# Four chained image layers on one core: channel squares added on GpSimd, row lengths sent through DRAM, first tokens moved among the first row's units

## The chip, the core and the metric

One core of one Trainium2 chip runs the whole program. The metric is device microseconds (us) for one execution, the median of several; lower is better. The engines are TensorE (PE, with its weight loads as PEld), VectorE (DVE), ScalarE (ACT), GpSimd (POOL) and SyncE (SP), which issues almost all DMAs of this kernel.

## The reference, cut to what matters

Four images of 56 x 56 tokens with 256 channels pass through four layers, each `x = x + layer(groupnorm(x))`. Layers 0, 2 and 3 are windowed attentions. The change lies in layer 1, a graph step in which every token of an image looks at every other one:

```python
x  = groupnorm(x)                                  # per image, n = 3136 tokens, c = 256
xn = x / maximum(norm(x, axis=-1), EPS)            # each token to unit length
A  = einsum('bnc,cc,bmc->bnm', xn, W_adj, xn)      # n x n per image
A  = exp(5 * (A - max(A)));  A = A * (1 - eye(n))
A  = A / maximum(sum(abs(A)), EPS)
xW = einsum('bnc,dc->bnd', x, W_aff)
diff = rowsum * (xW + b_aff) - A @ x @ W_aff.T
y  = leaky(layernorm(diff) * ln_gamma + ln_beta)   # then x = x + y
```

## The kernel before: tiles, queues and hand-written order

Data is float32 and lies with channels on partitions, as two halves of 128 channels (`CC = 2`). Layer 1 cuts an image into 24 tiles of 128 tokens and a rest of 64. Token preparation works on chunks of four tiles (512 tokens): chunks 0 to 5, and chunk 6, which holds the rest of this image (128 columns). The product A is symmetric, so only its upper triangle is made: a row `j` of tiles is a sequence of units `(b, j, first, last)` of up to four tiles. One unit is: logits (`logits`, L1409, 128x512), exponential (L1412, ACT), transposes (L1500, copied at L1503), and for each tile one product by row (L1514, summed in PSUM over the row) and one by column (L1519), which DVE adds to `acc` (L1441). Units of the rest have no `j` (L1451, L1470, L1480, L1484).

Preparing one chunk is the function `tokens(b, c)`, which returns steps:

- `load` (L1347): DMA of the chunk from DRAM to `x0`.
- `normal(h)` for both channel halves: group normalisation on DVE (L939), and after the second half the square of both halves on ACT (L1356, 128x1024), which overwrites `x0`.
- `values(i0)`: tokens times `W_aff` on PE (L1377), two tiles at a time, copied to `xw` by ACT (L954) and DVE (L952) in turn.
- `lengths`: the sum of squares of each token, by 1-column matmuls of the squares with ones, one for each tile and each channel half (L1364); then a floor on DVE (L1366), the power -1/2 on POOL (L1367) and a diagonal matrix `dg` on POOL (L1368).
- `unit_length`: one 128x512 matmul of ones with `dg` (L1385), which leaves each token's reciprocal length on all partitions, and the multiplication into `xnT` on DVE (L1387). `scaled(j)` (L1402, POOL) then makes the weighted tile `xd` for row j.

Where these steps stand is written by hand. Layer 1 runs under a manual schedule for PE and DVE: both execute in exactly the order in which the Python code issues the work[...]. ACT, POOL and SP are put in order by a scheduler. Three lists drive it:

- `small`: entries (when, step, chunk). `small_step` is called twice in each unit and runs the first entry whose `when` is not above `done`, the count of tiles processed.
- `ticks`: steps run one at a time after a product by column, behind the `due` steps of finished rows (L1573, L1578).
- `ready(chunk)`: called before a step of a chunk is taken from `small`; it issues at once whatever of the chunk's two `normal` steps still waits in `ticks`.

For images 1 to 3, `replace(b + 1, c)` is called at the start of rows 3, 6, 10, 14, 16, 19 and 23 of the image before (for chunks 6, 0, 1, 2, 3, 4, 5). It issues the load, appends four empty ticks and the two `normal` steps to `ticks`, and puts the other steps at the front of `small`:

```python
ticks.extend([no_step] * 4 + normals[b, c])
small[:0] = [(done + 12, step, (b, c)) for step in steps]
# steps: values(0), lengths, values(2), unit_length
```

For image 0 all seven chunks are prepared ahead of the first unit, in a loop, with PSUM tiles borrowed from tags v, o, t and s. Two rest units come first, then row 0. At the end of layer 0 the SP queue also fetches tables for layer 2: `w_wqkv` (L881, 768 KB) and two halves of `bias` (L1726, 3024 KB each).

Of the kernel before, what the change touches and what calls it, by code (L numbers as in the profile page):

```python
# [24 lines left out]
FP = mybir.dt.float32  # L25
I32 = mybir.dt.int32
AF = mybir.ActivationFunctionType
ALU = mybir.AluOpType
# [3 lines left out]
NIMG = 4  # L32
# [3 lines left out]
P = 128  # L36
CC = C // P
# [14 lines left out]
TINY = 1e-12  # L52
# [778 lines left out]
def direct_blocks(ctx: ExitStack, tc: tile.TileContext, d: dict, watch):  # L831
# [3 lines left out]
    nc = tc.nc  # L835
    const = ctx.enter_context(tc.tile_pool(name="dconst", bufs=1))
    dram = ctx.enter_context(tc.tile_pool(name="ddram", bufs=1, space=bass.MemoryType.DRAM))
    ps = None
    no_step = lambda: None
# [16 lines left out]
    ident = const.tile([P, P], FP, name="ident")  # L856
    make_identity(nc, ident)
    ones = const.tile([P, P], FP, name="ones")
    nc.vector.memset(ones, 1.0)
    mhalf = const.tile([P, CC], FP, name="mhalf")  # L860
# [9 lines left out]
    def psum_tile(tag, bufs, banks=1):  # L870
        shape = [P, 512] if banks == 1 else [P, banks, 512]
        return ps.tile(shape, FP, tag=tag, name="ps_" + tag, bufs=bufs)
# [447 lines left out]
    def layer1(early, big, pool, late, next_layer):  # L1320


        NB, REST = divmod(T, P)
        NC4 = NB // 4
# [5 lines left out]
        xnT = big.tile([P, CC, (NB + 1) * P], FP, name="xnT")  # L1330
        xw = big.tile([P, NB + 1, C + 1], FP, name="xw")
        xdr = big.tile([P, CC, P], FP, name="xdr")
        offd = big.tile([P, P], FP, name="offd")
        nc.vector.tensor_scalar(offd, ident, -1.0, 1.0, ALU.mult, ALU.add)
        nc.vector.memset(xw[:, :, C:], -1.0)

        def tokens(b, c, ps_a=ps_m):

            tiles = range(4 * c, min(4 * c + 4, NB + 1))
            k, m = P, len(tiles)  # L1340
            n = m * P
            box = {}

            def load():
                x = box["x0"] = early.tile([P, CC, 512], FP, tag="x", name="x1")
                if c < NC4:
                    nc.sync.dma_start(out=x[:, :, :n], in_=tokens_of(1, b, 4 * c * P, n))  # L1347
                else:
                    for i in range(2):
                        nc.sync.dma_start(out=x[:, :, i * REST:(i + 1) * REST], in_=tokens_of(1, b, NB * P, REST))  # L1350
                box["x"] = early.tile([P, CC, 512], FP, tag="xn", name="xn1")

            def normal(h):
                normalise(box["x"][:, h, :n], box["x0"][:, h, :n], known(1, b), h)
                if h:
                    nc.scalar.activation(box["x0"][:, :, :n], box["x"][:, :, :n], AF.Square)  # L1356

            def lengths():
                pm, sq = ps_a(), box["x0"]
                rn = early.tile([P, 4, 1], FP, tag="rn", name="rn")  # L1360
                dg = box["dg"] = early.tile([P, 4, P], FP, tag="dg", name="dg", bufs=1)
                for i, t in enumerate(tiles):
                    for h in range(CC):
                        nc.tensor.matmul(pm[:k, i:i + 1], lhsT=sq[:, h, i * P:i * P + k], rhs=ones[:, 0:1],  # L1364
                                         start=(h == 0), stop=(h == CC - 1))
                nc.vector.tensor_scalar_max(rn[:k, :m, 0], pm[:k, :m], TINY * TINY)  # L1366
                nc.gpsimd.tensor_tensor(rn[:k, :m, 0], rn[:k, :m, 0], mhalf[:k, 0:1].to_broadcast([k, m]), ALU.pow)  # L1367
                nc.gpsimd.tensor_tensor(  # L1368
                    dg[:k, :m, :k], ident[:k, :k].rearrange("p (o q) -> p o q", o=1).to_broadcast([k, m, k]),
                    rn[:k, :m, :].to_broadcast([k, m, k]), ALU.mult)  # L1370

            def values(i0):
                pm = ps_a()
                mm = min(2, m - i0)
                for i in range(i0, i0 + mm):
                    for h in range(CC):
                        nc.tensor.matmul(pm[:k, (i - i0) * C:(i - i0 + 1) * C], lhsT=box["x"][:, h, i * P:i * P + k],  # L1377
                                         rhs=w_aff[:, h, :], start=(h == 0), stop=(h == CC - 1))
                evac(i0 // 2, xw[:k, 4 * c + i0:4 * c + i0 + mm, :C],
                     pm[:k, :mm * C].rearrange("p (a b) -> p a b", b=C))  # L1380

            def unit_length():

                pm = ps_a()
                nc.tensor.matmul(pm[:, :n].rearrange("p (m k) -> p m k", k=k), lhsT=ones[:k, :], rhs=box["dg"][:k, :m, :k],  # L1385
                                 start=True, stop=True)
                nc.vector.tensor_tensor(xnT[:, :, 4 * c * P:4 * c * P + n], box["x"][:, :, :n],  # L1387
                                        pm[:, :n].rearrange("p (o k) -> p o k", o=1).to_broadcast([P, CC, n]), ALU.mult)
                if c == NC4:
                    for h in range(CC):  # L1390
                        nc.gpsimd.tensor_scalar_mul(xdr[:, h, :], xnT[:, h, NB * P:], adj[:, h:h + 1])

            return [load], [lambda h=h: normal(h) for h in range(CC)], [lambda: values(0), lengths] + [lambda i=i: values(i) for i in range(2, m, 2)] + [unit_length]

        xd, out, xr = {}, {}, {}
        y_rest = late.tile([REST, C + 1], FP, name="yr", bufs=1)

        def scaled(j):

            xd[j] = pool.tile([P, CC, P], FP, tag="xd", name="xd", bufs=3)  # L1400
            for h in range(CC):
                nc.gpsimd.tensor_scalar_mul(xd[j][:, h, :], xnT[:, h, j * P:(j + 1) * P], adj[:, h:h + 1])  # L1402
# [206 lines left out]

        units = []  # L1610
        for b in range(NIMG):
            if b == 0:
                units += [(b, None, q) for q in range(2)]
            for j in range(NB):
                units += [(b, j, i, min(i + 4, NB)) for i in range(j, NB, 4)]
                if j == 0:
                    units.append((b, None, 2))
                if b + 1 < NIMG and 0 <= j - 20 < 2:
                    units.append((b + 1, None, j - 20))
        turn = iter(range(6 * (NC4 + 1)))  # L1620
        fresh = [tokens(0, c, lambda: psum_tile(*(("v", 2), ("o", 2), ("t", 1), ("s", 2))[next(turn) % 4])) for c in range(NC4 + 1)]
        for c in range(2):
            fresh[c][0].pop()()
        for step in fresh[0][1]:
            step()
        for c in range(NC4 + 1):
            for step in (fresh[c + 1][1] if c < NC4 else []) + fresh[c][2]:
                step()
            if c + 2 <= NC4:
                fresh[c + 2][0].pop()()  # L1630
        small, done = [], 0

        normals = {}

# [6 lines left out]
        def small_step():  # L1641
            for i, (when, step, chunk) in enumerate(small):
                if when <= done:
                    small.pop(i)
                    if chunk and chunk != -1:
                        ready(chunk)
                    return step()
            step_stats()
# [8 lines left out]
        def replace(b, c):  # L1657
            if b < NIMG:
                for item in [a[2] for a in small if a[2] not in (None, -1)]:
                    now(item)  # L1660
                (load,), normals[b, c], steps = tokens(b, c)
                load()
                ticks.extend([no_step] * 4 + normals[b, c])
                small[:0] = [(done + 12, step, (b, c)) for step in steps]

        def begin(w):
            if w[1] is None:
# [7 lines left out]
        e = begin(units[0])  # L1675
        for k, w in enumerate(units):
            b, j, first = w[:3]
            if first == j:
                residual(b, j * P // CH)
                residual(b, j * P // CH + 1)  # L1680
                if j in begin_at:
                    replace(b + 1, begin_at[j])
                if (b, j) == (NIMG - 2, 8):
                    small += [(done + 20, step, None) for step in next_layer()]
            small_step()
            at = transposed(*w, e) if j is not None else rest_transposed(e[0])
            if k + 2 < len(units) and units[k + 2][1] == units[k + 2][2]:
                scaled(units[k + 2][1])
            ahead = begin(units[k + 1]) if k + 1 < len(units) else None
            small_step()  # L1690
            if j is None:
                rest_products(b, first, *e, at)
                done += 4
                if first == NC4 // 2 - 1:
                    last_add = finish(b, NB)
            else:
                products(*w, e, at)
                done += w[3] - first
                if w[3] == NB:
                    finish(b, j)  # L1700
            e = ahead
# [555 lines left out]
```

## Time and profile before

| | |
|---|---|
| median of 3 runs | 3989.01 us |
| lowest and highest run | 3976.07 and 3992.41 us |
| profiled execution: span, first to last instruction | 3977.8 us |
| mean granted TensorE clock in the span | 0.983 |
| PE busy in the span | 3814.5 us (96%) |
| DVE, POOL, ACT busy in the span | 2372.2, 1745.8, 1381.2 us |
| layer 1: first to last matmul, about | 803 to 2754 us |
| 880 to 2700 us: PE busy | 1809.5 of 1820 us |

No separate total is given for the profiled execution; its span is 1.7 us above the lowest timed run and 11.2 us below the median. In rows of the profile, a time such as `1.00` under PEclk is the granted clock as a share of full speed, `xN` is the number of instructions, and `[a <-E tile Lnnn]` is idle time of that engine before the instruction and what ended it. A float32 matmul is recorded as two instructions[...], so eight 1-column matmuls show as x16.

### The profile page before, as it was taken

To read this page: it belongs to the slowest core of one execution; us is meant where nothing else is said; L and a number is where in the kernel's file an instruction comes from. 1 tells how busy PE (TensorE), PEld (TensorE's weight loads), DVE (VectorE), ACT (ScalarE), POOL (GpSimd) and SP (SyncE) were. 2 spreads that over 40 slices of the span, in tenths; PEclk is the share of its full clock that TensorE was granted. 3 is DMA by queue.
4 is the path that set the end of the run, shared out by engine and by line. 5 is a ranking of instruction groups with operands and counts; after the bars stand their busy time and mean duration, and the time that the engine had idled before them with its cause. 6 is when DMAs were issued, how large, how long until landed. Compare 5 with 4: busy or idle time off the path is not lost. (4 is left out here: it accounts for less than half of the span.)

```text
span 3977.8 us, 92350 instructions
## 1 busy us (share of the span) xinstructions
PE 3814.5 (96%) x38871; PEld 2707.4 (68%) x38871; DVE 2372.2 (60%) x4431; ACT 1381.2 (35%) x2927; POOL 1745.8 (44%) x1883
## 2 busy tenths in 40 slices
PE   7999999889999999999999999999999999899998
PEld 4566666557777677776777767776676666566765
DVE  6777777734345544445444553446788887666665
ACT  3455545422222222222222222222555555344443
POOL 3566767721123312233112331123677777555554
PEclk9899999989999999999999999999999999999999
DMA  8343333320000100001000000001344443434442
GB/s 270 104 134 119 113 120 104 99 104 1 24 19 24 40 6 15 20 25 35 6 24 15 25 24 10 10 10 56 111 125 126 125 121 111 157 120 135 127 128 93
DMA packets 268659, 301.84 MB, mean 76 GB/s; under 512 B 25926, under 2 KB 260584, under 8 KB 267752
## 3 DMA queue, kind: packets, MB, share of 16 engines
q1 hardware_dynamic: 267946, 295.76, 23.9%
q8 instruction: 308, 5.05, 0.5%
q14 instruction: 117, 0.96, 0.1%
q10 hardware_dynamic: 288, 0.08, 0.0%
HBM read 203.39 MB, written 92.37 MB: 74 GB/s over the span
## 5 line engine op out<-in xcount | busy, mean ns | idle before, releaser
L1441 DVE TENSOR_TENSOR acc<-acc,ps_v 128x257 f32<-128x257 f32 x1104 | 463.4, 423 | 718.7 <-PE ps_v L1519 690.7
L1519 PE MATMUL ps_v<-xw,e 128*128 128x257 f32 x2208 | 612.6, 382 | 1.2 <-DVE acc L1441 1.2
L1514 PE MATMUL ps_o<-xw,at 128*128 128x257 f32 x2208 | 609.0, 379 | 0.0
L1409 PE MATMUL ps_s<-xnT,xd 128*128 128x512 f32 (+3 forms) x1344 | 572.7, 549 | 3.9 <-DVE xnT L1387 3.9
L1519 PEld LDWEIGHTS ps_v<-xw,e 128*128 128x128 f32 x2208 | 413.5, 189 | 142.7 <-issue 82.4
L1503 ACT COPY at<-ps_t 128x512 f32<-128x512 f32 (+3 forms) x332 | 170.6, 514 | 970.0 <-PE ps_t L1500 969.7
L1078 POOL TENSOR_TENSOR b<-e 126x336 f32<-126x336 f32 (+5 forms) x512 | 500.0, 997 | 9.6 <-ACT e L1066 1.5
L1514 PEld LDWEIGHTS ps_o<-xw,at 128*128 128x128 f32 x2208 | 419.1, 190 | 60.1
L945 PE MATMUL ps_m<-xn,w_wqkv 128*128 128x392 f32 x1024 | 379.1, 504 | 12.3 <-DVE dv L922 3.9
L1402 POOL TENSOR_SCALAR xd<-xnT,vec 128x128 f32<-128x128 f32 x192 | 116.8, 619 | 569.3 <-PE ps_s L1409 565.7
L1069 POOL TENSOR_TENSOR e<-e,m0t 126x672 f32<-126x672 f32 (+3 forms) x128 | 238.6, 1864 | 265.8 <-ACT e L1068 245.4
L1069 POOL TENSOR_TENSOR e<-e,bias 119x784 f32<-119x784 f32 (+5 forms) x128 | 244.0, 1906 | 179.9 <-ACT e L1068 178.6
L1409 PEld LDWEIGHTS ps_s<-xnT,xd 128*128 128x128 f32 x1344 | 225.8, 191 | 141.8 <-issue 126.5
L1412 ACT ACTIVATE e<-ps_s 128x512 f32<-128x512 f32 x336 | 185.4, 552 | 347.8 <-PE ps_s L1409 340.8
L990 ACT ACTIVATE no<-rs 128x168 f32<-128x168 f32 (+2 forms) x256 | 93.8, 367 | 583.8 <-DVE rs L1841 268.3
L945 PEld LDWEIGHTS ps_m<-xn,w_wqkv 128*128 128x128 f32 x1024 | 187.8, 191 | 137.3 <-ACT pr L2097 17.5
L1087 PEld LDWEIGHTS ps_o<-e,vp 124*32 124x32 f32 (+3 forms) x8192 | 177.8, 111 | 147.4 <-issue 97.7
L1087 PE MATMUL ps_o<-e,vp 124*32 124x112 f32 (+3 forms) x8192 | 242.0, 254 | 6.2 <-POOL e L1069 4.4
L1841 DVE RECIPROCAL rs<-ps_o 128x196 f32<-128x196 f32 (+2 forms) x128 | 176.0, 1375 | 87.1 <-PE ps_o L1087 86.6
L939 DVE TENSOR_SCALAR xn<-x,gst 128x28 f32<-128x28 f32 (+4 forms) x368 | 207.5, 616 | 32.3 <-PE ps_m L945 22.9
L1066 ACT ACTIVATE e<-e 126x672 f32<-126x672 f32 (+5 forms) x256 | 219.5, 857 | 20.7 <-DVE e L1065 8.0
L1019 POOL TENSOR_TENSOR e<-e,m3l 98x784 f32<-98x784 f32 x64 | 118.3, 1848 | 217.9 <-ACT e L1016 217.9
(196 smaller groups left out, 6293.8 us busy)
## 6 DMA issues: line engine op xcount, KB each, us to landing
x<-xr SPq DMA_DIRECT2D x64, 392.0 KB
x<-in_x SPq DMA_DIRECT2D x53, 448.0 KB
x<-x SPq DMA_DIRECT2D x60, 392.0 KB
xr<-x SPq DMA_DIRECT2D x60, 392.0 KB
vd<-v SPq DMA_DIRECT2D x72, 256.0 KB
xr<-in_x SPq DMA_DIRECT2D x32, 392.0 KB
xr<-x SPq DMA_DIRECT2D x28, 448.0 KB
x<-xr SPq DMA_DIRECT2D x28, 448.0 KB
```

Of the source, the lines that this page charges most:

```text
L939: nc.vector.tensor_scalar(dst, src, gst[:, h, 0:1], gst[:, h, 1:2], ALU.subtract, ALU.mult)
L945: nc.tensor.matmul(pm[:, :n], lhsT=w[:, h, col:col + P], rhs=rhs(h), start=(h == 0), stop=(h == CC - 1))
L1066: nc.scalar.activation(ev, ev, AF.Exp)
L1069: nc.gpsimd.tensor_tensor(parts(ev), parts(ev), w["emask"], ALU.mult)
L1078: nc.gpsimd.tensor_tensor(w["b"][a][:nk, :, :2 * nq].rearrange("p h (i c) -> p h i c", i=2), ev[:, :, :, 0, :], ev[:, :, :, 1, :], ALU.add)
L1087: nc.tensor.matmul(w["o"](k, i)[j * HD:(j + 1) * HD], lhsT=ones[:nk, :HD] if k else v(j, u), rhs=w["b"][j // 2][:nk, j % 2, i * nq:(i + 1) ...
L1409: nc.tensor.matmul(s[:, :n], lhsT=xd[j][:, h, :], rhs=xnT[:, h, first * P:last * P], start=(h == 0), stop=(h == CC - 1))
L1412: nc.scalar.activation(e[:, :n], s[:, :n], AF.Exp, scale=5.0)
L1441: nc.vector.tensor_tensor(acc[:, i, :], acc[:, i, :], pv[:, :C + 1], ALU.add)
L1514: nc.tensor.matmul(out[j][:, :C + 1], lhsT=e[:, col(i)] if i == j else at[:, col(i)], rhs=xw[:, i, :], start=(i == j), stop=(i == NB - 1))
L1519: nc.tensor.matmul(pv[:, :C + 1], lhsT=e[:, col(i)], rhs=xw[:, j, :], start=True, stop=True)
L1841: nc.vector.reciprocal(rs.rearrange("p (t c) -> p t c", t=2), pv[:, :, 1, :])
```

## The change

Four edits to layer 1:

1. `normal`: after the square, POOL adds the second half of the squares to the first (new L1359, 128x512). `lengths` then needs one 1-column matmul for each tile, not two (L1365).
2. `lengths` no longer makes the diagonal matrix. It writes the reciprocal lengths (128 partitions x 4) to a DRAM buffer `shares` (L1369), 4 bytes at a time, and reads them back as a row of 512 repeated on all partitions, `share` (L1371). Both DMAs are on SP, and the second waits for the first. `unit_length` has no matmul and multiplies by `share` from SBUF (L1385).
3. Order of a chunk's steps: `lengths`, `values(0)`, `values(2)`, an empty step, `unit_length`; and in `replace` they are due at `done + 8`, not `done + 12`.
4. Image 0: only chunks 0 and 1 are prepared ahead of the first unit (chunk 1 without its `unit_length`). The steps of the others, their `normal` steps and loads among them, go into `small`, and six further `small_step` calls are made at the start of each of the first six units. Chunk 6 comes before chunk 5, and the rest units stand after five, six and six units of row 0.

```diff
@@ normal
-                    nc.scalar.activation(box["x0"][:, :, :n], box["x"][:, :, :n], AF.Square)
+                    sq = box["x0"]
+                    nc.scalar.activation(sq[:, :, :n], box["x"][:, :, :n], AF.Square)
+                    nc.gpsimd.tensor_tensor(sq[:, 0, :n], sq[:, 0, :n], sq[:, 1, :n], ALU.add)
@@ lengths
-                for i, t in enumerate(tiles):
-                    for h in range(CC):
-                        nc.tensor.matmul(pm[:k, i:i + 1], lhsT=sq[:, h, i * P:i * P + k], rhs=ones[:, 0:1],
-                                         start=(h == 0), stop=(h == CC - 1))
-                nc.vector.tensor_scalar_max(rn[:k, :m, 0], pm[:k, :m], TINY * TINY)
-                nc.gpsimd.tensor_tensor(rn[:k, :m, 0], rn[:k, :m, 0], mhalf[:k, 0:1].to_broadcast([k, m]), ALU.pow)
-                nc.gpsimd.tensor_tensor(
-                    dg[:k, :m, :k], ident[:k, :k].rearrange("p (o q) -> p o q", o=1).to_broadcast([k, m, k]),
-                    rn[:k, :m, :].to_broadcast([k, m, k]), ALU.mult)
+                for i in range(m):
+                    nc.tensor.matmul(pm[:, i:i + 1], lhsT=sq[:, 0, i * P:(i + 1) * P], rhs=ones[:, 0:1], start=True, stop=True)
+                nc.vector.tensor_scalar_max(rn[:, :m], pm[:, :m], TINY * TINY)
+                nc.gpsimd.tensor_tensor(rn[:, :m], rn[:, :m], mhalf[:, 0:1].to_broadcast([P, m]), ALU.pow)
+                row = shares[b:b + 1, 4 * c * P:4 * c * P + n]
+                nc.sync.dma_start(out=row.rearrange("o (m p) -> p (o m)", p=P), in_=rn[:, :m])
+                box["share"] = early.tile([P, 512], FP, tag="share", name="share", bufs=1)
+                nc.sync.dma_start(out=box["share"][:, :n], in_=row.to_broadcast([P, n]))
@@ unit_length
-                pm = ps_a()
-                nc.tensor.matmul(pm[:, :n].rearrange("p (m k) -> p m k", k=k), lhsT=ones[:k, :], rhs=box["dg"][:k, :m, :k],
-                                 start=True, stop=True)
                 nc.vector.tensor_tensor(xnT[:, :, 4 * c * P:4 * c * P + n], box["x"][:, :, :n],
-                                        pm[:, :n].rearrange("p (o k) -> p o k", o=1).to_broadcast([P, CC, n]), ALU.mult)
+                                        box["share"][:, :n].rearrange("p (o k) -> p o k", o=1).to_broadcast([P, CC, n]), ALU.mult)
@@ what tokens returns
-            return [load], [...], [lambda: values(0), lengths] + [... values(i) for i in range(2, m, 2)] + [unit_length]
+            return [load], [...], [lengths, lambda: values(0)] + [... values(i) for i in range(2, m, 2)] + [no_step, unit_length]
@@ units of image 0
-            if b == 0:
-                units += [(b, None, q) for q in range(2)]
                 if j == 0:
+                    if b == 0:
+                        units.insert(-1, (b, None, 0))
+                        units.append((b, None, 1))
                     units.append((b, None, 2))
@@ image 0's chunks (the loop over all seven is replaced)
+        first = [*range(NC4 - 1), NC4, NC4 - 1]
+        for i, c in enumerate(first):
+            _, normal, (lengths, *rest) = fresh[i]
+            steps = [(0, step, (0, c)) for step in normal + [lengths]]
+            if i > 1:
+                steps.append((0, fresh[i - 1][2][-1], (0, first[i - 1])))
+            steps += [(0, step, (0, c)) for step in rest[:-2]]
+            if i + 2 < len(first):
+                steps.append((0, fresh[i + 2][0][0], (0, c)))
+            if i < 2:
+                for _, step, _ in steps:
+                    step()
+                if i == 0:
+                    rest[-1]()
+            else:
+                small += steps
+        small.append((0, fresh[-1][2][-1], (0, first[-1])))
+        scaled(0)
@@ replace
-                small[:0] = [(done + 12, step, (b, c)) for step in steps]
+                small[:0] = [(done + 8, step, (b, c)) for step in steps]
@@ loop over units
+            for _ in range(6 if k < NC4 else 0):
+                small_step()
```

More of the change, by code (lines that the diff above doesn't have):

```diff
@@ L1332, in layer1 @@
         xdr = big.tile([P, CC, P], FP, name="xdr")
+        shares = dram.tile([NIMG, (NB + 1) * P], FP, name="shares")
         offd = big.tile([P, P], FP, name="offd")
@@ L1355, in normal @@
                 if h:
-                    nc.scalar.activation(box["x0"][:, :, :n], box["x"][:, :, :n], AF.Square)
+                    sq = box["x0"]
+                    nc.scalar.activation(sq[:, :, :n], box["x"][:, :, :n], AF.Square)
+                    nc.gpsimd.tensor_tensor(sq[:, 0, :n], sq[:, 0, :n], sq[:, 1, :n], ALU.add)
             def lengths():
                 pm, sq = ps_a(), box["x0"]
-                rn = early.tile([P, 4, 1], FP, tag="rn", name="rn")
-                dg = box["dg"] = early.tile([P, 4, P], FP, tag="dg", name="dg", bufs=1)
-                for i, t in enumerate(tiles):
-                    for h in range(CC):
-                        nc.tensor.matmul(pm[:k, i:i + 1], lhsT=sq[:, h, i * P:i * P + k], rhs=ones[:, 0:1],
-                                         start=(h == 0), stop=(h == CC - 1))
-                nc.vector.tensor_scalar_max(rn[:k, :m, 0], pm[:k, :m], TINY * TINY)
-                nc.gpsimd.tensor_tensor(rn[:k, :m, 0], rn[:k, :m, 0], mhalf[:k, 0:1].to_broadcast([k, m]), ALU.pow)
-                nc.gpsimd.tensor_tensor(
-                    dg[:k, :m, :k], ident[:k, :k].rearrange("p (o q) -> p o q", o=1).to_broadcast([k, m, k]),
-                    rn[:k, :m, :].to_broadcast([k, m, k]), ALU.mult)
+                rn = early.tile([P, 4], FP, tag="rn", name="rn")
+                for i in range(m):
[6 more added lines that the diff above has]
+                nc.sync.dma_start(out=box["share"][:, :n], in_=row.to_broadcast([P, n]))
             def values(i0):
@@ L1391, in unit_length @@
                         nc.gpsimd.tensor_scalar_mul(xdr[:, h, :], xnT[:, h, NB * P:], adj[:, h:h + 1])
-            return [load], [lambda h=h: normal(h) for h in range(CC)], [lambda: values(0), lengths] + [lambda i=i: values(i) for i in range(2, m, 2)] + [unit_length]
+            return [load], [lambda h=h: normal(h) for h in range(CC)], [lengths, lambda: values(0)] + [lambda i=i: values(i) for i in range(2, m, 2)] + [no_step, unit_length]
         xd, out, xr = {}, {}, {}
@@ L1619, in layer1 @@
                     units.append((b + 1, None, j - 20))
-        turn = iter(range(6 * (NC4 + 1)))
-        fresh = [tokens(0, c, lambda: psum_tile(*(("v", 2), ("o", 2), ("t", 1), ("s", 2))[next(turn) % 4])) for c in range(NC4 + 1)]
-        for c in range(2):
[L1623 to L1631, printed above, removed]
+        small, done = [], 0
+        turn = iter(range(8))
+        first = [*range(NC4 - 1), NC4, NC4 - 1]
+        fresh = [tokens(0, c, *([lambda: psum_tile(*(("v", 2), ("o", 2), ("t", 1), ("s", 2))[next(turn) % 4])] if c < 2 else []))
+                 for c in first]
+        for c in range(2):
+            fresh[c][0][0]()
+        for i, c in enumerate(first):
[15 more added lines that the diff above has]
+        scaled(0)
         normals = {}
```

## The prediction, made before the changed kernel had run

> **What bounds the kernel now.** I read the busy shares first, then busy time by stretch over layer 1, then the timeline around one chunk of tokens and around the start of the layer. In the stretch below, the columns are time, length, busy PE, PEld, DVE, ACT, POOL, granted clock, DMA share and GB/s.
>
> ```profile
> 1020.00:2340.00 1320.00, 1311.27 (x5917) 965.32 (x5916) 616.93 (x1593) 288.16 (x538) 345.12 (x532) 1.00 0.07 22
> ```
>
> PE is busy 99% at full clock and DVE 47%: through images 1 to 3 of layer 1, what is taken from PE shortens the kernel and any wait of PE lengthens it, one for one. Now one chunk's preparation for image 1:
>
> ```profile
> 1176.16 0.54 DVE L939 TENSOR_SCALAR xn<-x,gst 128x512 f32<-128x512 f32 x1
> ...
> 1178.98 0.54 DVE L939 TENSOR_SCALAR xn<-x,gst 128x512 f32<-128x512 f32 x1
> ...
> 1179.55 1.06 ACT L1356 ACTIVATE x<-xn 128x1024 f32<-128x1024 f32 x1 [0.90 <-DVE xn L939]
> ...
> 1181.48 1.89 PE L1377 MATMUL ps_m<-w_waff,xn 128*128 128x256 f32 x8
> ...
> 1185.14 1.84 PE L1364 MATMUL ps_m<-ones,x 128*128 128x1 f32 x16
> ...
> 1186.84 1.11 PE L1519 MATMUL ps_v<-xw,e 128*128 128x257 f32 x4
> 1187.02 0.16 DVE L1366 TENSOR_SCALAR rn<-ps_m 128x4 f32<-128x4 f32 x1 [5.79 <-PE ps_m L1364]
> ...
> 1188.39 1.04 POOL L1368 TENSOR_TENSOR dg<-ident,rn 128x512 f32<-128x512 f32 x1
> ```
>
> The squares are ready at 1180.61 and PE reaches the 1-column matmuls only at 1185.14: they come 4.5 us late and so never wait. That slack is what the change spends. The start of the layer is looser:
>
> ```profile
> 821.94 1.12 PE L1385 MATMUL ps_s<-dg,ones 128*128 128x512 f32 x2 [2.19 <-POOL dg L1368]
> ...
> 854.42 0.49 PE L1385 MATMUL ps_t<-dg,ones 128*128 128x128 f32 x2 [1.91 <-POOL dg L1368]
> 856.13 4.26 PE L1451 MATMUL ps_s<-xnT,xdr 128*64 128x512 f32 x8 [1.22 <-POOL xdr L1391]
> ```
>
> From 803.1 us (first matmul of the layer) to 920.4 us (row 1 begins) PE idles 8.8 us by such brackets, and runs at half clock from 804 to 814 and 855 to 865 us.
>
> [...] Two idle gaps of PE (in brackets), then the stretches behind them, columns as above:
>
> ```profile
> 428.11 2.62 PE L945 MATMUL ps_m<-attn,w_wo 128*128 128x392 f32 x4 [3.65 <-DVE attn L1239]
> ```
> ```profile
> 2757.19 5.49 PE L971 MATMUL ps_m<-w_wqkv,xn 128*128 128x256 f32 x12 [3.14 <-DVE xn L939]
> ```
> ```profile
> 428.00:432.00 4.00, 3.89 (x36) 2.31 (x40) 2.01 (x4) 1.61 (x4) 3.00 (x3) 0.57 0.28 102
> ...
> 2756.00:2760.00 4.00, 2.81 (x7) 2.28 (x8) 3.93 (x15) 0.20 (x1) 1.30 (x2) 0.55 0.66 224
> 2760.00:2764.00 4.00, 3.33 (x9) 2.08 (x8) 3.18 (x5) 0.00 (x0) 3.80 (x6) 0.60 0.68 209
> ```
>
> After 3.65 us idle, 4 x 0.43 = 1.7 us of full-speed work is lost; after 3.14 us, 4 x (0.45 + 0.40) = 3.4 us, part of it while idle. All nine gaps over 2.6 us that I looked up elsewhere are followed by a 0.50 stretch; the 1.3 us gaps in layer 1 mostly are not.
>
> [...]
>
> ```profile
> 802.86 0.51 SPq L1726 DMA_DIRECT2D bias<-in_bias  x1
> 809.41 8.94 SPq L1347 DMA_DIRECT2D x<-x  x2
> ```
> ```profile
> 1025.34 0.36 SPq L1597 DMA_DIRECT2D x<-xr  x1
> 1028.33 0.36 SPq L1542 DMA_DIRECT2D xr<-x  x1
> ```
>
> A 512 KB load issued at 809.41 behind the bias table has its bytes only by 814.9, when the traffic falls to 4 GB/s. The second pair: a load that waits for a 448 KB store to land is issued 2.6 us after it.
>
> **The change, images 1 to 3: what it removes.** Eight 1-column matmuls take 1186.84 - 1185.14 = 1.70 us of PE; half go: 0.85. The broadcast matmul L1385 takes 0.86 (1096.59 to 1097.45). That is 1.71 for a full chunk, 0.4 for chunk 6: 6 x 1.71 + 0.4 = 10.7 an image, **-32 us** for three, all on the path. POOL loses the diagonal (1.04) and gains the addition (taken as the same 1.04; two bounds: 0.73, the 128x256 L1574, and 1.27, the slowest diagonal).
>
> **What the new order adds.** I followed the built program's order. Chunks become due at `done + 8`, two units after `replace`. In two units there are 7 ticks; four are empty and two or so go to the finished row's due steps, so the `normal` steps are mostly still in `ticks`. `lengths` is now the first step, so `ready` issues them right then. For all 21 chunks of images 1 to 3, DVE has the last normalisation behind the last column addition of the unit (or behind the row's closing steps), while PE has the 1-column matmuls directly after that unit's last two row products. They then wait for DVE, ACT and POOL in series. PE is in order: transposes, logits and products of the next unit queue behind.
>
> From the start of the last column product (1175.18 in a typical unit): its addition ends at +1.06 (1176.24), two normalisations +1.0, hand-over and square 0.08 + 1.06, hand-over and addition 0.08 + 1.04, hand-over 0.07: +4.39. PE is free at +1.31 (1176.49). Wait **3.08 us**, chunks 0, 1, 2. Chunk 5 has one normalisation left: 2.58. Chunks 3 and 4 stand behind a row's closing steps (1165.98 to 1167.99, ending 2.21 after PE is free): with one normalisation 2.21 + 0.54 + 1.14 + 1.12 + 0.07 = 5.08, with two 5.58. Chunk 6 (two of 0.3, square 0.42, addition 0.46): 1.46. One image: 3 x 3.08 + 2.58 + 5.08 + 5.58 + 1.46 = 23.9; three: **+72 us**.
>
> **Clock.** 18 of these waits exceed 2.5 us. At the nearest gaps the loss was 1.7 to 3.4 us, less what fell in the idle time: I take 2.3, and nine in ten hit: 16 x 2.3 = **+37** (0 to 61).
>
> **Round trip.** After `lengths`: floor 0.16, power 1.04, store 0.4 to issue and 2.6 to land, load the same: about 7.5 us with hand-overs. The trace shows no 4-byte store; below it cannot be under the issue, above I allow 6 us. PE work between `lengths` and `unit_length` is 11.4 to 14.3 us for full chunks, 5.6 for chunk 6: covered, except 1 us or so at chunk 6 on DVE. If the store took over 4 us more, DVE would stop on `share` with column additions queued behind it, and PE after two of those. SP holds the loads and stores of the residual behind the two waits; those have tens of microseconds. I take 0 (0 to +30).
>
> **Image 0.** Gone with the old loop: -10.7 of matmuls; of the 8.8 idle and about 9.3 lost to the clock, new ones take the place. `lengths` of chunk 0 starts at 805.8, not 803.1: normalisations end 803.5, square and addition 2.3. Its store is issued about 808.5 behind `bias`, done near 813.5; it lands near 816. But SP has meanwhile issued x (512 KB) and the second half of `bias` (3024 KB), and the load of `share` stands behind them: 3.6 MB at 0.41 MB/us, so it arrives near 825. `unit_length` of chunk 0 waits for it on DVE, and behind it the normalisation of chunk 1; on POOL six scalings (3.9) stand ahead of chunk 1's addition. So 825 + 1.2 + 3.9 + 1.2 = 831.3 for chunk 1's matmuls. PE has had 4.3 us of full-speed work in 25.5: 21.2 lost. Then half clock 4; waits at the next chunks' `lengths` of 1.8, 2.3 and 3.2 by the chain above; the statistics step 1.8; rest units with both additions on DVE 1.5; clock 3.5. Remaining work was 117.3 - 8.8 - 9.3 - 10.7 = 88.5. End: 805.8 + 88.5 + 39.3 = 933.6 against 920.4: **+13** (from -4, if the small read passes the table, to +25).
>
> **Sum.** -32 + 72 + 37 + 13 = +90. Against the span of 3977.8 that is 4068; the median lies 11 us above that span, and I state the forecast against it: 3989 + 90 = **4079 us**.
>
> **The rivals.** (a) *Waits without clock loss.* For it: at 1.3 us gaps the clock usually stays. Against: all gaps of this size lost it. 4079 - 37 = 4042. (b) *The round trip shows too*, a slow 4-byte store: 2 us at 18 chunks, 4115; nothing in the trace speaks for it but the store is unlike any shown. (c) *Faster: the waits are covered.* Place: the 1-column matmuls of images 1 to 3. If DVE, ACT and POOL get the squares done while PE finishes its row products, the 32 us stay and image 0 costs 13: 3970, with a good image 0 3953. It decides below about 1 us of wait for each full chunk, (32 - 13) / 18. Against it: the serial chain alone (1.0 + 1.06 + 1.04) is over three times that, and only 0.87 us of row products covers it.
>
> **Chances.** Forecast 0.64, (a) 0.14, (b) 0.09, (c) 0.08, the rest a smaller loss near no change. A difference under 0.5% (20 us) is about what a measurement of this kernel cannot tell from none. Forecast and (a) give slower; so does (b): slower 0.87, same 0.07, faster 0.06. The range takes in (a) and most of (b): 4030 to 4125; low is no clock loss with a mild image 0 (-32 + 72 + 0 - 4 = +36, rounded up for some clock loss), high is all 18 gaps at the upper clock price and image 0 at +25, +126, and some noise.
>
> **What would show it.** Right: idle of PE before L1365 ended by POOL's L1359, 2.5 to 5.6 us each in images 1 to 3, some 72 us together; clock at 0.5 after them; DVE not waiting for `share` there; PE idle some 15 us near 815 to 831. Wrong: L1365 with little idle before it, or L1385 on DVE waiting for DMA in images 1 to 3.

## The result: slower by 3.8%, and the profile after

The changed kernel takes 4131.0 us (median of 5 runs) against 3976.8 us for the kernel before in the same session: a ratio of 1.038, 95% interval 1.036 to 1.040. (Two more runs of the kernel before have moved its median from the 3989.0 us that the forecast started from.) The direction was forecast; the size was not: +148 us between the two profiled spans (3977.8 and 4126.0), where +90 had been worked out and the range ended at 4125.

The first view is again the busy time of layer 1 by stretch (time, length, busy PE, PEld, DVE, ACT, POOL, granted clock, DMA share, GB/s):

```profile
1020.00:2340.00 1320.00, 1246.42 (x5336) 914.99 (x5335) 559.64 (x1446) 268.32 (x495) 310.94 (x468) 0.96 0.09 22
```

PE is down from 99% to 94% busy, its clock from 1.00 to 0.96. The waits are found by asking what each matmul of a line waited for. In images 1 to 3, for the 1-column matmuls (L1365) and the products by column (L1517), in us and times:

```profile
  POOL x L1359: 70.8, 21
```
```profile
  DVE acc L1439: 17.1, 9
```

In the kernel before, no 1-column matmul waited there, and the products by column (L1519) hardly:

```profile
  DVE acc L1441: 1.2, 3
```

The first wait was forecast, the second not. One chunk of image 1 shows both chains in the timeline:

```profile
1124.72 1.00 DVE L939 TENSOR_SCALAR xn<-x,gst 128x512 f32<-128x512 f32 x2
1125.75 1.06 ACT L1358 ACTIVATE x<-xn 128x1024 f32<-128x1024 f32 x1 [3.37 <-DVE xn L939]
1126.89 1.26 POOL L1359 TENSOR_TENSOR x<-x 128x512 f32<-128x512 f32 x1 [6.64 <-ACT x L1358]
1128.20 1.86 PE L1365 MATMUL ps_m<-ones,x 128*128 128x1 f32 x8 [2.99 <-POOL x L1359]
...
1131.39 0.36 SPq L1369 DMA_DIRECT2D shares<-rn  x1
...
1139.49 0.33 SPq L1371 DMA_DIRECT2D share<-shares  x1
...
1145.55 1.22 DVE L1385 TENSOR_TENSOR xnT<-xn,share 128x1024 f32<-128x1024 f32 x1
```

Normalisation, square and addition follow each other without a pause while PE stands idle for 2.99 us. Then the store of the lengths leaves at 1131.39, and the load that waits for it leaves only at 1139.49, 8.1 us later. Here DVE comes to the multiplication late enough not to stop. For the small chunk 6 it does stop, with additions to `acc` behind it, and PE behind those:

```profile
1048.19 0.42 DVE L1385 TENSOR_TENSOR xnT<-xn,share 128x256 f32<-128x256 f32 x1 [7.05 <-DMA share<-shares]
...
1049.00 1.23 PE L1517 MATMUL ps_v<-xw,e 128*128 128x257 f32 x2 [4.00 <-DVE acc L1439]
```

Image 0, same view, from the store of chunk 0's lengths to the matmuls of chunk 1:

```profile
808.10 0.37 SPq L1369 DMA_DIRECT2D shares<-rn  x1
808.57 0.45 SPq L1348 DMA_DIRECT2D x<-x  x1
809.07 0.48 SPq L1739 DMA_DIRECT2D bias<-in_bias  x1
...
821.86 0.33 SPq L1371 DMA_DIRECT2D share<-shares  x1
830.29 1.22 DVE L1385 TENSOR_TENSOR xnT<-xn,share 128x1024 f32<-128x1024 f32 x1 [17.64 <-DMA share<-shares]
831.43 1.05 DVE L939 TENSOR_SCALAR xn<-x,gst 128x512 f32<-128x512 f32 x2
831.62 3.91 POOL L1400 TENSOR_SCALAR xd<-xnT,vec 128x128 f32<-128x128 f32 x6 [20.00 <-DVE xnT L1385]
...
835.50 1.26 POOL L1359 TENSOR_TENSOR x<-x 128x512 f32<-128x512 f32 x1
836.81 1.44 PE L1365 MATMUL ps_s<-ones,x 128*128 128x1 f32 x6 [24.89 <-POOL x L1359]
```

A ledger of layer 1 makes the sum. It is cut at the last matmul of layer 0, at the rest-by-rest product (L1488, now L1486) in each image's last rest unit, and at the layer's last matmul. *Idle* is time in which PE runs no matmul. *Clock* is half of PE's busy time inside the stretches that the trace gives as 0.50, an estimate (the four 1-column matmuls of a chunk take 1.86 us in such a stretch, at 1128.20, and 1.05 at 1.00, at 1309.39). *Work* is what remains.

| stretch | before: length, idle, clock, work | after: length, idle, clock, work |
|---|---|---|
| image 0 | 118.6, 10.7, 9.4, 98.5 | 159.2, 50.9, 18.8, 89.5 |
| to image 1's last rest unit | 484.1, 3.5, 0.0, 480.6 | 520.4, 32.0, 17.7, 470.6 |
| to image 2's | 485.8, 3.5, 1.7, 480.6 | 522.3, 30.8, 20.9, 470.6 |
| to image 3's | 484.1, 3.5, 0.0, 480.6 | 522.4, 31.5, 20.3, 470.6 |
| rest of the layer | 380.2, 0.1, 0.0, 380.1 | 380.2, 0.1, 0.0, 380.1 |

The layer takes 1952.8 us before and 2104.4 after; the other layers differ by 3.3 us in all, the other way.

### The profile page after: what moved, and what is told of

It is laid out like the page before. It is cut to its first block, busy times and chain, and to the rows that moved or that the text cites. A ratio compares the mean times of both kernels' runs of the same rounds, so it can differ in the third digit from the quotient of the medians.

```text
span 4126.0 us, 91945 instructions
## 1 busy us (share of the span) xinstructions
PE 3837.6 (93%) x38615; PEld 2716.4 (66%) x38615; DVE 2373.4 (58%) x4439; ACT 1380.4 (33%) x2919; POOL 1761.0 (43%) x1883
## 5 line engine op out<-in xcount | busy, mean ns | idle before, releaser
L1517 PE MATMUL ps_v<-xw,e 128*128 128x257 f32 x2208 | 614.0, 383 | 17.1 <-DVE acc L1439 17.1
L1407 PE MATMUL ps_s<-xnT,xd 128*128 128x512 f32 (+3 forms) x1344 | 596.5, 568 | 1.2 <-DVE xnT L1385 1.2
L1517 PEld LDWEIGHTS ps_v<-xw,e 128*128 128x128 f32 x2208 | 415.1, 190 | 160.0 <-issue 81.3
L1407 PEld LDWEIGHTS ps_s<-xnT,xd 128*128 128x128 f32 x1344 | 234.6, 198 | 143.9 <-issue 134.4
L1068 ACT ACTIVATE e<-ps_s 126x672 f32<-126x672 f32 (+5 forms) x256 | 206.1, 805 | 18.1 <-PE ps_s L1058 18.0
```

The costliest lines, as they stand in the source:

```text
L1068: nc.scalar.activation(ev, sv, AF.Exp)
L1407: nc.tensor.matmul(s[:, :n], lhsT=xd[j][:, h, :], rhs=xnT[:, h, first * P:last * P], start=(h == 0), stop=(h == CC - 1))
L1517: nc.tensor.matmul(pv[:, :C + 1], lhsT=e[:, col(i)], rhs=xw[:, j, :], start=True, stop=True)
```

## The experiments

Ratios are to the kernel before in the same session, with a 95% interval; parts are read from the same ledger. Three theories were to be told apart: waits for a serial chain flushed at the last moment (the forecast), a round trip slower than its cover, and image 0's order.

**1. Normal steps early.** In `replace` of the changed kernel:

```diff
-                ticks.extend([no_step] * 4 + normals[b, c])
+                ticks.extend(normals[b, c])
```

> The changed kernel with one edit: the two normal steps of a chunk enter the ticks without the four empty ones ahead, so DVE normalises some four column products earlier; all due dates stay. Theory A (lengths waits for the chain normalisation, square, addition only because the normalisations are flushed at the last moment): the idle time before the 1-column matmuls in images 1 to 3, 70.8 us in the changed kernel's trace, falls to under 3, and the half-clock stretches behind those waits go with it, about 50 of 59 us. The waits for the shares (some 20 us) and image 0 stay: 4131 - 71 - 50 = 4010. Rival B (the clock falls for another reason, or the waits for the shares now cost the clock): only the idle goes, about 4060. Rival C (POOL's queue holds the addition back): waits stay, 4131.

Measured: 4038.5 us, ratio 1.015 (1.012 to 1.018), 28 us above theory A and some 21 below rival B. The first line is for the 1-column matmuls, the second for the products by column, images 1 to 3:

```profile
  POOL x L1359: 1.4, 3
```
```profile
  DVE acc L1439: 31.0, 12
```

The wait for the chain is gone, 70.8 to 1.4, by moving two DVE instructions, so rival C is out. But the idle time of the products by column and of the rest (L1478) that stands behind a stop of DVE for shares rises from 14.4 to 36.3 us. (In the changed kernel these products idle for 4.7 us more, while DVE is at other work.) Clock losses in images 1 to 3 fall from 58.9 to 19.1, and all nine half-clock stretches that are left stand behind such waits: here rival B has a part. Two things come into question for their growth. At chunks 3 and 4, where 16.7 of the 36.3 us fall, the lengths now come while a row's closing steps hold DVE and POOL, and the store leaves 4.5 to 4.7 us after them, not 1.3. The other is the half clock behind each wait of the changed kernel: it lies between a chunk's store and its use; without it PE comes to the shares sooner. Experiment 9 tries the second.

**2. No round trip.** The changed kernel with `dg`, its matmul and the multiplication from PSUM put back:

```diff
-                nc.sync.dma_start(out=row.rearrange("o (m p) -> p (o m)", p=P), in_=rn[:, :m])
-                nc.sync.dma_start(out=box["share"][:, :n], in_=row.to_broadcast([P, n]))
+                nc.gpsimd.tensor_tensor(dg[:, :m, :], ident..., rn[:, :m]..., ALU.mult)
...
+                nc.tensor.matmul(pm[:, :n]..., lhsT=ones, rhs=box["dg"][:, :m, :], start=True, stop=True)
```

> The changed kernel with the round trip through DRAM taken back: POOL makes the diagonal matrix again and one matmul with ones spreads the reciprocal lengths; addition on POOL, order and due dates of the changed kernel stay. Theory A (the round trip costs image 0 most: chunk 1 and the last chunks wait for shares there, and costs images 1 to 3 the idle before the column products): idle before the column products of images 1 to 3, 17 of the 20 us, goes; PE gains 24 broadcast matmuls of 0.86, 21 us; the 24.9 us gap of image 0 shrinks to under 8 and its 7.7 and 4.2 gaps to under 3: about 4131 - 17 - 8 clock + 21 - 30 = 4097. The waits before the 1-column matmuls of images 1 to 3 stay near 71 us. Rival B (the gap of image 0 is the order of the steps, not the round trip): the 24.9 gap stays over 15, time 4120 to 4131.

Measured: 4114.8, ratio 1.033 (1.031 to 1.035), 18 above theory A. The large gap of image 0 did shrink, from 24.89 to this:

```profile
830.30 1.86 PE L1366 MATMUL ps_v<-ones,x 128*128 128x1 f32 x8 [6.56 <-POOL x L1359]
```

Yet image 0 takes 144.5 us: 14.7 less than with the round trip, and still 25.9 more than before. That part is the new order itself. In images 1 to 3 the waits before the 1-column matmuls stay (71.2 us), those of the column products nearly go (2.2), and 9.1 us are new: transposes of finished rows wait for DVE to read the spread lengths out of the one PSUM buffer `ps_m`. The same 18 waits cost less clock here, 41.9 us against 51.8 (58.9 without the 7.1 behind waits for shares).

**3. The addition alone.** The kernel before with the addition on POOL and one 1-column matmul for each tile, nothing else.

```diff
+                    nc.gpsimd.tensor_tensor(sq[:, 0, :n], sq[:, 0, :n], sq[:, 1, :n], ALU.add)
...
-                    for h in range(CC):
-                        nc.tensor.matmul(pm[:k, i:i + 1], lhsT=sq[:, h, i * P:i * P + k], rhs=ones[:, 0:1], ...)
+                    nc.tensor.matmul(pm[:k, i:i + 1], lhsT=sq[:, 0, i * P:i * P + k], rhs=ones[:, 0:1], ...)
```

> The kernel before with only the addition of the squares' halves on POOL and one 1-column matmul for each tile; order, due dates, diagonal matrix and image 0 as before. Theory A (the addition by itself is a gain where the lengths matmuls have slack): 18 full chunks x 0.85 and a little for the small ones = -16 us in images 1 to 3, no idle before the 1-column matmuls there; in image 0 -5 from matmuls, at most +5 from POOL's longer chain: 3977 - 16 = 3961 (3955 to 3968). Rival B (the addition itself makes PE wait, since the slack of 4.5 us is used by POOL's other work): idle appears before the 1-column matmuls, 3977 or more.

Measured: 3959.8, ratio 0.9945 (0.9925 to 0.9964), as theory A. No 1-column matmul of images 1 to 3 waits, and PE's work falls from 480.6 to 475.1 an image. Edit 1 is a gain where the matmuls have slack.

**4. Tables late.** The changed kernel; a write of DVE into the bias tile, in its place in image 2, holds the two table loads back:

```diff
+            nc.vector.memset(bias[:, 2 * a:2 * a + 2, 0:1], 0.0)
             nc.sync.dma_start(out=bias[:, 2 * a:2 * a + 2, :], in_=d["bias2"][:, 2 * a:2 * a + 2, :])
```

> The changed kernel with the two 3024 KB bias loads of layer 2 held back to image 2 by a one-element write of DVE into their tiles. Theory A (in image 0 the first load of shares stands behind the second half of the table): it is issued about 8 us after the store and lands 4.4 us later, as the others, near 820.5 instead of 830.3; the 24.9 us gap of PE falls to about 15, image 0 ends 10 to 13 us earlier: 4119. Rival B (the order of the steps and the round trip alone make the gap): no change, 4131.

Measured: 4122.0, ratio 1.035 (1.033 to 1.037). Image 0 takes 146.4, 12.8 less, and its gap is 16.1 us. The load of shares waits only for its own store now, and still 9.1 us:

```profile
812.39 0.36 SPq L1369 DMA_DIRECT2D shares<-rn  x1
821.49 0.34 SPq L1371 DMA_DIRECT2D share<-shares  x1
```

**5. Hidden round trip.** Addition on POOL; image 0 as before the change, with `dg`; for images 1 to 3 the round trip, normal steps early, due at `done + 8`, and

```diff
-[lengths, lambda: values(0)] + [lambda i=i: values(i) for i in range(2, m, 2)] + [no_step, unit_length]
+[lengths, lambda: values(0)] + [lambda i=i: values(i) for i in range(2, m, 2)] + [no_step] * 3 + [unit_length]
```

> Addition on POOL, the kernel before's order for image 0 with the diagonal matrix there; for images 1 to 3 the round trip through DRAM, due 8 tiles after the row that starts a chunk, normal steps early as in the first experiment, and three empty steps ahead of unit_length in place of one, one unit (5.6 us) more time for the shares. Theory A (the round trip costs PE only what is not covered, some 12 to 14 us after lengths): no idle before column products in images 1 to 3; against the experiment with the addition alone, 18 broadcast matmuls of 0.86 are gone, about -16: 3960 - 16 = 3944 (3936 to 3952). Rival B (the waits come from DVE or SP standing still for another cause, such as the loads behind the waits in SP's queue): idle before column products stays, 6 us or more for each image, 3965 or more.

Measured: 3941.6, ratio 0.9904 (0.9888 to 0.9919). Idle before the column products is 1.4 us in three images, idle in all 3.3 to 4.5 an image, work 468.2 to 468.5, clock loss none. Theory A. One unit more between store and use is all that PE needed; DVE still stops for shares nine times, 0.4 to 2.0 us, and PE notices almost nothing of it (0.2 us).

**6. Row store.** As 5, but the lengths are turned on PE, in a step of their own, and stored in rows:

```diff
-                nc.sync.dma_start(out=row.rearrange("o (m p) -> p (o m)", p=P), in_=rn[:, :m])
+                nc.tensor.transpose(pt[:m, :P], rn[:, :m], ident)
+                nc.scalar.copy(rows[:m, :], pt[:m, :P])
+                nc.sync.dma_start(out=row.rearrange("o (m p) -> (o m) p", p=P), in_=rows[:m, :])
```

> As the hidden round trip, but the reciprocal lengths are turned on PE (128x4 to 4x128) and copied by ACT in a step of their own, and stored as 4 pieces of 512 bytes, not 512 of 4 bytes. It measures what the store's 8 us from its issue to the issue of the dependent load consist of. Theory A (many small writes to DRAM are what is slow): it falls to about 3 us, as behind the 448 KB stores (2.7). Rival B (a fixed time, or the 512 KB load just ahead in the queue): it stays at 7 to 8.5 us. Time in both cases within 10 us of the hidden round trip, 3944 to 3954, as the shares are covered.

Measured: 3938.8, ratio 0.9901 (0.9883 to 0.9918), the same as 5. The store with its dependent load, and beside it the last one of the changed kernel, where no load stands close ahead of it in the queue:

```profile
1086.11 0.27 SPq L1382 DMA_DIRECT2D shares<-rows  x1
1087.29 0.34 SPq L1384 DMA_DIRECT2D share<-shares  x1
```
```profile
2486.69 0.36 SPq L1369 DMA_DIRECT2D shares<-rn  x1
2495.89 0.33 SPq L1371 DMA_DIRECT2D share<-shares  x1
```

1.2 us against 9.2: the same 2 KB, in 4 pieces or 512. Not even theory A's 3 us remain, and a load ahead in the queue is not what makes 8 us. The number of pieces is not the whole of it: chunk 6 stores 128 of them and its load leaves 8.0 us after (1035.85 to 1043.81). The row store also leaves from 4 partitions in place of 128; whether the size of a piece, a number between 4 and 128 or the partitions decide was not tried.

**7. Image 0 ahead.** As 5, with the changed kernel's interleaved image 0, but two chunks prepared ahead and

```diff
-            steps = [(0, step, (0, c)) for step in normal + [lengths]]
+            steps = [(0, step, (0, c)) for step in (fresh[i + 1][1] if i + 1 < len(first) else []) + fresh[i][2]]
```

> As the hidden round trip for images 1 to 3; image 0 with the changed kernel's order of units, its chunks among the units of row 0, but the normal steps one chunk ahead of lengths (two chunks prepared ahead of the first unit) and the diagonal matrix, no round trip. Theory A (what the new order of image 0 costs is lengths waiting for its own chunk's normalisation, square and addition, issued right ahead of it): the stretch up to the last rest unit of image 0, 118.6 us before, 159.2 in the changed kernel and 144.5 in it without the round trip, falls to 108 to 120; 3938 to 3950. Rival B (among the units the clock or PSUM buffers cost as much): 135 or more, 3965 or more.

Measured: 3941.0, ratio 0.9909 (0.9894 to 0.9923). Image 0 takes 117.9 us: theory A. With a chunk's normalisations issued one chunk ahead, the interleaved order hardly stops PE at lengths (0.6 us once, the first chunk apart); in experiment 2, with them right ahead of lengths, PE waited 2.5 to 6.6 us at four of them, and image 0 took 144.5. (A chunk's `unit_length` also stands among its own steps here, no longer among those of the next; that was not tried apart.) Interleaving itself gains nothing measurable over the order before (115.3 in experiment 5).

**8. Row store in the changed kernel.** Experiment 1 with the turned store of 6 in all images.

```diff
-[lengths, lambda: values(0)] + [lambda i=i: values(i) for i in range(2, m, 2)] + [no_step, unit_length]
+[lengths, lambda: values(0), turned] + [lambda i=i: values(i) for i in range(2, m, 2)] + [no_step, unit_length]
```

> The first experiment (normal steps early) with one more edit, in all images: the reciprocal lengths are turned on PE in a step of their own behind values(0), copied by ACT and stored as 4 pieces of 512 bytes. Order, dates and the one empty step stay. Theory A (the share waits of the changed kernel are the slow landing of 512 small writes and nothing else): the load of shares is issued 1.2 us after the store, not 8; the idle before column products in images 1 to 3, 11 to 12.7 us an image in the first experiment, falls under 2 and 5 to 9 us of clock loss an image with it: images 1 to 3 some 50 us shorter; image 0 5 to 15 us shorter, as its first load of shares stays behind the table: 4038 - 60 = 3978 (3968 to 3990). Rival B (the step comes later now, so the shares are as late as before): idle stays over 6 us an image, 4010 or more.

Measured: 3977.9, ratio 0.9987 (0.9973 to 1.0001), as theory A. What the column products still wait for:

```profile
  DVE acc L1446: 2.3, 3
```

Images 1 to 3 take 473.4 to 473.5 us each, idle 3.5, no clock loss. The order and the one empty step are those of the changed kernel. The step that turns the lengths gives chunk 6 more time behind them (DVE is free after 11.8 us, not 6.1), but the store too leaves later: from store to a free DVE there are 5 to 8 us, where experiment 1 had 5 to 13 and stopped. So the share waits were the slow landing of the store: its load leaves 1.2 us after it here (1126.84 to 1128.08), 8.1 in the changed kernel. The rest of the loss is image 0, 143.9.

**9. PE kept busy.** The changed kernel with matmuls ahead of the 1-column ones in images 1 to 3; nothing reads their product.

```diff
+                for _ in range({3: 5, 4: 5, NC4: 1}.get(c, 3) if b else 0):
+                    nc.tensor.matmul(pm, lhsT=ones, rhs=w_aff.rearrange("p h n -> p (h n)"), start=True, stop=True)
```

> The changed kernel with matmuls ahead of the 1-column matmuls in images 1 to 3 whose product nobody reads (ones with w_aff, 128x512, 0.86 us each: 3 for chunks 0, 1, 2 and 5, 5 for chunks 3 and 4, 1 for chunk 6), so that PE works through most of each wait and is late by as much as before. It separates the clock from the wait. Theory A (the half-clock stretches behind the waits are a cost of their own on top of the waits, 15 to 18 us an image): idle before the 1-column matmuls falls from 23.6 to 3 or 4 us an image, the half-clock stretches behind lengths go, the lengths matmuls themselves start no later: 4131 - 3 x 16 = 4083 (4072 to 4095). Rival B (the half clock in the records costs nothing, since PE waits for others there anyway): 4131, or more by what the extra matmuls delay.

Measured: 4110.0, ratio 1.033 (1.032 to 1.035): 27 above theory A, though not 4131. A wait in the timeline, the same stretch by windows (columns as in the first view), and what the 1-column matmuls and the column products waited for:

```profile
1126.83 2.74 PE L1365 MATMUL ps_m<-w_waff,ones 128*128 128x512 f32 x6
1129.98 1.05 PE L1367 MATMUL ps_m<-ones,x 128*128 128x1 f32 x8 [0.41 <-POOL x L1359]
```
```profile
1127.00:1134.00 7.00, 6.58 (x27) 3.74 (x27) 0.66 (x3) 2.24 (x3) 2.28 (x2) 1.00 0.25 65
```
```profile
  POOL x L1359: 11.7, 21
```
```profile
  DVE acc L1441: 31.8, 12
```

The clock stays at 1.00 where the changed kernel, in about the same stretch, had 0.50:

```profile
1127.30:1134.10 6.80, 5.90 (x16) 3.96 (x17) 0.16 (x1) 0.59 (x1) 1.87 (x2) 0.50 0.30 77
```

Over images 1 to 3 clock losses fall by 42.3 us, from 58.9 to 16.6; of these, some 13 stand behind waits for shares. So the clock is here a cost of its own. But PE now reaches the column products sooner: DVE stops for shares 16 times in place of 6, and PE waits behind that 29.9 us in place of 14.4. Of the 42 us only 24 are left in the layer's time (2104.4 to 2080.3): under slow matmuls part of the round trip had been hidden.

## Why the prediction was right in direction and short by 58 us

Measured terms come from the ledger; the share waits are the idle time of PE behind a stop of DVE for shares (six times, at chunks 6 and 2), their clock loss that of the three stretches behind chunk 6 (1.6 + 2.8 + 2.7). The second figure taken off the clock, 1.7, was lost before the change too.

| term of the sum | predicted | measured |
|---|---|---|
| PE work removed, images 1 to 3 | -32 | -30.0 |
| waits before the 1-column matmuls | +72 | +70.8 |
| clock behind those waits | +37 | 58.9 - 7.1 - 1.7 = +50.1 |
| round trip, waits and their clock | 0 | 14.4 + 7.1 = +21.5 |
| other idle time of images 1 to 3 | 0 | 9.1 - 10.5 = -1.4 |
| image 0 | +13 | +40.6 |
| outside layer 1 | 0 | -3.3 |
| sum | +90 | +148 |

Of the 58 us, 27 are image 0, 21 the round trip and 13 the clock; the other terms take some 4 back. Of these three, only image 0 left the bounds that the forecast gave it (-4 to +25; 0 to +30 and 0 to 61 for the others).

- **What the new order adds: right.** 2.99 us for 3.08 (chunks 0 to 2), 4.98 for 5.08, 5.46 for 5.58, 3.05 for 2.58, 1.14 for 1.46. The addition took 1.26 us, the upper of its two bounds, where 1.04 had been put, but a normalisation that overlaps the addition to `acc` and a PE that is free 0.15 us later made up for it. Experiment 1 shows that the cause is the late flush, experiment 3 that it is not the addition.
- **Clock: right that these waits lose it, the size too small.** All 18 waits lost the clock, not 16, at 51.8 / 18 = 2.9 us in place of 2.3. The half-clock stretches behind them are 3.4 or 6.8 us long. Why equal waits brought the longer one more often in the changed kernel than in experiment 2 was not settled. The loss is also not simply additive (experiment 9: 42.3 us less of it, 24 us less time).
- **"Round trip ... I take 0": wrong.** From the end of the lengths to the use of the shares 7.5 us had been put; where DVE stops for them, the changed kernel shows 12.6 to 14.7. The price of landing was read from a 448 KB store, whose dependent load leaves 3.0 us after the store's issue began (2.6 after it ended); behind the store of 4-byte pieces it leaves after 7.4 to 9.4 in images 1 to 3. At chunk 6 that is 8.0, and DVE has the shares 4.4 us after the load's issue (1043.81 to 1048.19): 12.3 us stand where 6 had been put, and floor and power come ahead of them. The cover was read about rightly: DVE is free for the multiplication 6.1 us after the lengths of chunk 6 (put at 5.6), and 11.9 to 16.8 us after those of full chunks in experiment 1 (11.4 to 14.3). It is no longer enough, for chunk 6 least of all: 11.1 of the 14.4 us stand there. At full chunks the forecast's own waits and half clock stretch the cover to 13.6 to 19.1 us, and only chunk 2 still stops. The rival of a slow 4-byte store had named the cause, at 2 us for each of 18 full chunks and a chance of 0.09; it came on top of the forecast, and for the most part at chunk 6.
- **Image 0: "+13" wrong in size, though its first step held.** The load did stand behind the table (experiment 4), DVE and POOL did stop in the order given, and chunk 1's matmuls came at 836.8 for 831.3; from the layer's first matmul to there 27.4 us were lost to idle time and clock, where 21.2 had been put. The larger miss comes behind: 37.6 us (21.2 idle, 16.4 clock), where 18.1 had been put (10.6 and 7.5). Waits of 7.65 us before the last full chunk, 5.1 at the statistics and 3.3 at `values` were not in the sum or were too small there. Undoing the table gives 12.8 us back, undoing the whole round trip 14.7; the other 25.9 us are the order, which puts each chunk's chain right ahead of its own lengths.
- **What was removed: right.** Experiments 3 and 5 show the two halves, 5.5 and 6.7 us of work an image; in the changed kernel itself it is 10.0, for 10.7 put.

## What to carry to other kernels

Edit 1 alone was a gain where its operands were early (ratio 0.9945, experiment 3); in the changed kernel, where they were late, PE waited 70.8 us for them. So with a cheaper instruction look at who makes them, how many engines they pass in series, and what in the order forces them to the last moment. Price a new DMA by one with as many pieces of the same size from as many partitions, not by one of the same queue (here 2 KB in 512 pieces of 4 bytes let the dependent load go after 8.1 us, a 448 KB store on the same queue after 3.0), and give a round trip cover that does not consist of another stall. Repair one wait and read the others again before adding up what is left, for here a clock slowed by one wait hid part of the next: with 42.3 us less lost to the clock, the share waits rose from 14.4 to 29.9 (experiment 9).

## What the runs showed of the hardware

- A store of 2 KB to DRAM in 512 pieces of 4 bytes let its dependent load go 8.1 us after its own issue (9.2 at the last one, where no load stood close ahead in the queue), in 128 pieces 8.0 us, and as 4 pieces of 512 bytes after 1.2 us. In the traffic of the chunk shown above (columns of half a microsecond from 1128) all but some 90 bytes of the load ahead and the store have passed by 1133.5, and next to nothing moves for 7.5 us; the dependent load leaves 6 us into that:

```profile
GB/s 0 0 0 0 0 0 102 123 344 393 90 0 0 0 0 0 0 0 0 0 0 0 0 0 0 0 41 25 106 172 78 102 0 0 33 0 0 0 0 0
```

- Gaps of a few microseconds cost the clock here: each of the 18 waits of 2.98 to 5.46 us did, the three of 1.14 did not. In between and even below 1.3 us it went either way: 1.92 us cost it twice and 1.52 did not (L1478, experiment 1), 1.31 cost it once in three times (L1409, before the change), 1.17 or 1.18 twice in three (L1367, experiment 9). A PE kept at work by matmuls that nobody reads held its clock at 16 of the 18 waits, and lost 42 us less in all. That is no repair; with the operand in time (experiment 1) the wait was gone as well, 1.4 us in place of the changed kernel's 70.8.
